# Forward transform of a Fourier layer: row differences moved to GpSimd, table scalings to ScalarE, table pieces handed out anew

## The chip, the cores and the metric

The kernel runs on one core of a Trainium2 chip, in one launch. The metric is the device time of the whole launch in microseconds. Its instructions go to five engines, each with a queue of its own that is worked off strictly in order: TensorE (PE, matmuls; PEld is its weight load), VectorE (DVE), ScalarE (ACT), GpSimd (POOL) and SyncE (SP), which only issues DMAs. All data are 32-bit floats.

## The reference

The input `x` has 16 images of 16 channels of 256 x 256. Two residual layers follow each other. The change lies in the first one, which, cut to its core, is this:

```python
x = x + _L0_conv_ref(_gn(x), ...)          # group norm over 8 groups, then:
alpha = jnp.fft.fft2(x, axes=(-2, -1))
A  = 1.0 / (omega1[:, None, None, None] - weights_pole1[None])   # [256, 16, 16, 4]
Bm = 1.0 / (omega2[:, None, None, None] - weights_pole2[None])
S  = jnp.einsum('ikpq,oikp,xikq->oxik', weights_residue, A, Bm)
output_residue1 = jnp.einsum('biox,oxik->bkox', alpha, S)
C  = jnp.einsum('biox,oikp->bikpx', alpha, A)
D  = jnp.einsum('bikpx,xikq->bikpq', C, Bm)
output_residue2 = jnp.einsum('bikpq,ikpq->bkpq', D, weights_residue)
x1 = jnp.fft.ifft2(output_residue1, ...).real
E1 = jnp.exp(weights_pole1[..., None] * tyc)   # and E2 alike; x2 is built from them
return x1 + x2 / Nx / Ny
```

The second layer is an involution block with a 3 x 3 convolution and a channel gate. It takes most of the time and is untouched.

## The kernel before, in words

The kernel works in four stages, one after the other, with their intermediate results in device memory: `layer0_forward` (group norm, forward Fourier transform, products with the poles), `layer0_mix` (mixing of channels for each frequency), `layer0_back` (inverse transform) and `layer1`. Only `layer0_forward` and what it calls are changed.

**Steps.** `layer0_forward` goes through 64 steps (b, cg): 16 images, and in each 4 groups of 4 channels. In a step,

- `fetch` (two steps ahead) loads 4 channels, 1 MB, to `z`, and takes their statistics on VectorE (`bn_stats`, L174).
- `halves` (one step ahead) forms the group norm's scalars. They cross engines several times: TensorE averages over partitions (`gn_mean`, L34), VectorE does small operations (L36 to L39), TensorE averages again (`gn_var`, L42), then VectorE and ScalarE (square root, L46) make the scale. `eo` is the sum and the difference of the image's upper and lower half: the sum on VectorE (L191), the difference on GpSimd (L194, 128 x 1024).
- `rows`, called twice for two channels each, multiplies `eo` with the Fourier matrix `fy` (L207, into PSUM tile `pu`) and with the pole table `at` (L214, into `pv`). `pu` holds four products, for the left and right half of x and for even and odd frequencies. Left plus right and left minus right go to the two halves of `u`: ScalarE copies the right half to SBUF (`right`, L222), and VectorE adds and subtracts (L224, twice a channel). `u` keeps a whole image, with channels innermost, so each of these writes steps by 64 bytes. There are two `u`, one for the image being filled, one being read.
- `poles` multiplies with `bt` and the residues; `columns`, for the image before, transforms along x (L313), evicts on ScalarE (`o`, L320), and stores to `al` with DMAs issued from GpSimd (L329). `finish` closes an image.

**Tables.** `table` builds `at` before step 0 and `bt` in it. For each half of the channels it forms e = omega - Im(pole) on VectorE (L135, `q`), squares it, adds `p2` (the pole's real part squared, made by GpSimd, L131), takes the reciprocal and multiplies. `tables` builds what the later stages read, and stores it: 16 residue tables (`td`, with 8 matmuls each, L437), 33 plane tables (`avd`) and 16 pieces of exponentials (`ed`, two poles each; sine on ScalarE, exponential by a polynomial on VectorE). `tables` is a generator. `layer0_forward` calls it once at the end of each step from step 4 on; a call issues one residue table, or three planes, or one piece of exponentials, in this order, and the generator is spent before the steps are.

**Who sets the order.** In `layer0_forward` TensorE's order is the one in which the program is written (`manual_schedule` with PE alone). For VectorE, ScalarE, GpSimd and SP a planner places each instruction, using its own estimates of durations and of readiness; so an instruction can stand much earlier in its queue than in the text. In the later stages the order of the compute engines is written by hand. Most tiles of `tables` have one buffer (pools `tc` and `tp`), and PSUM tiles `pu`, `pv` and `px` have two each.

Of the kernel before, what the change touches and what calls it, by code (L numbers as in the profile page):

```python
# [10 lines left out]
F32 = mybir.dt.float32  # L11
I32 = mybir.dt.int32
AF = mybir.ActivationFunctionType
# [5 lines left out]
C = 16  # L19
# [4 lines left out]
M = 4  # L24
# [48 lines left out]
def layer0_forward(ctx, tc, d, al, bd, tabs):  # L73
# [47 lines left out]
    def table(axis, wx, w):  # L121

        t, planes = (at, (0, 1)) if axis == "1" else (bt, (1, 2, 0))
        for half in range(2):
# [5 lines left out]
            p2 = ap.tile([P, 512], F32, tag="p2", name="p2")  # L130
            nc.gpsimd.tensor_tensor(p2, pr, pr, ALU.mult)  # L131
            q = ap.tile([P, 2, 2, 512], F32, tag="q", name="q", bufs=2)
            for h in range(2):
                e, r = q[:, h, 1], q[:, h, 0]
                nc.vector.tensor_scalar(e, pi, -1.0, w[:, h : h + 1], ALU.mult, ALU.add)  # L135
                nc.vector.tensor_tensor(r, e, e, ALU.mult)
                nc.vector.tensor_tensor(r, r, p2, ALU.add)
                nc.vector.reciprocal(r, r)
                nc.vector.scalar_tensor_tensor(e, e, -1.0, r, ALU.mult, ALU.mult)
                nc.vector.scalar_tensor_tensor(r, pr, -1.0, r, ALU.mult, ALU.mult)  # L140
# [56 lines left out]
    def rows(b, cg, j, eo, rs):  # L197
# [3 lines left out]
        for a in range(2):  # L201
# [19 lines left out]
            right = ep.tile([P, 2, 2, 64], F32, tag="right", name="right")  # L221
            nc.scalar.copy(right, pu[:, 1])  # L222
            for h, sign in ((0, ALU.add), (1, ALU.subtract)):
                nc.vector.tensor_tensor(  # L224
                    u[:, h, :, :64, :, ch],
                    pu[:, 0].rearrange("p e v m -> p v m e"),
                    right.rearrange("p e v m -> p v m e"),
                    sign,
                )
# [106 lines left out]
    with tc.manual_schedule(engines={mybir.EngineType.PE}):  # L336
# [6 lines left out]
        for i, (b, cg) in enumerate(steps):  # L343
# [21 lines left out]
            if i >= 4:  # L365
                next(pieces, None)
# [16 lines left out]
def tables(ctx, tc, d, psum, tabs):  # L383
# [5 lines left out]


    krow = load(nc, cp, d["krow_t"], [P, N], "krow_t")
    w = frequencies(nc, cp, d["tx"], krow, [P, N], "wt")
    sign = load(nc, cp, d["sign_t"], [P, 1], "sign_t")
    qr = cp.tile([P, C], F32, name="tqr")
    qi = cp.tile([P, C], F32, name="tqi")
    rr = cp.tile([P, C, M], F32, name="trr")
    ri = cp.tile([P, C, M], F32, name="tri")
    for t in range(2):
        ps = slice(64 * t, 64 * t + 64)
        nc.sync.dma_start(out=qr[ps], in_=d["p2r_iq"])  # L400
        nc.sync.dma_start(out=qi[ps], in_=d["p2i_iq"])
        nc.sync.dma_start(out=rr[ps], in_=d["rr_iq"])
        nc.sync.dma_start(out=ri[ps], in_=d["ri_iq"])
    nc.vector.tensor_scalar(qi, qi, sign, None, ALU.mult)
    nri = cp.tile([P, C, M], F32, name="tnri")
    nc.vector.tensor_scalar(nri, ri, sign, None, ALU.mult)
    nc.vector.tensor_scalar(ri, nri, -1.0, None, ALU.mult)
    q2 = cp.tile([P, C], F32, name="tq2")
    nc.vector.tensor_tensor(q2, qr, qr, ALU.mult)
    mt = load(nc, cp, d["mt"], [P, 2, 16], "mt")  # L410
    for k in range(C):
        e = tp.tile([P, N], F32, tag="te", name="te")
        r = tp.tile([P, N], F32, tag="trec", name="trec")
        br = tp.tile([P, N], F32, tag="tbr", name="tbr")
        nc.vector.tensor_scalar(e, w, qi[:, k : k + 1], None, ALU.add)
        nc.vector.tensor_tensor(r, e, e, ALU.mult)
        nc.vector.tensor_scalar(r, r, q2[:, k : k + 1], None, ALU.add)
        nc.vector.reciprocal(r, r)
        nc.vector.tensor_scalar(br, r, qr[:, k : k + 1], -1.0, ALU.mult, ALU.mult)
        nc.vector.scalar_tensor_tensor(e, e, -1.0, r, ALU.mult, ALU.mult)  # L420
        wts = []
        for h in range(2):
            wt = tp.tile([P, 2, 2, 16, M], F32, tag=f"wt{h}", name="wt")
            shape = [P, 16, M]
            for part, c, coef in ((0, 0, rr), (0, 1, ri), (1, 0, nri), (1, 1, rr)):
                nc.vector.tensor_tensor(
                    wt[:, part, c],
                    mt[:, h].unsqueeze(2).to_broadcast(shape),
                    coef[:, k].unsqueeze(1).to_broadcast(shape),
                    ALU.mult,  # L430
                )
            wts.append(wt)
        yield
        ps = psum.tile([P, 2, N], F32, tag="px", name="pt")
        for h, wt in enumerate(wts):
            for part, rhs in ((0, br), (1, e)):
                nc.tensor.matmul(  # L437
                    ps[:, h],
                    lhsT=wt[:, part].rearrange("p c i m -> p (c i m)"),
                    rhs=rhs,  # L440
                    start=part == 0,
                    stop=part == 1,
                )
        t = tp.tile([P, 2, N], F32, tag="tt", name="tt")
        nc.scalar.copy(t, ps)
        nc.sync.dma_start(out=td[:, :, k], in_=t)

    krow = load(nc, cp, d["krow_m"], [P, N], "krow_m")  # L450
    w = frequencies(nc, cp, d["ty"], krow, [P, N], "wm")
    sign = load(nc, cp, d["sign_m"], [P, 1], "sign_m")
    pr = cp.tile([P, 32], F32, name="tpr")
    pi = cp.tile([P, 32], F32, name="tpi")
    for q in range(4):
        nc.sync.dma_start(out=pr[32 * q : 32 * q + 32], in_=d["p1r_ip"])
        nc.sync.dma_start(out=pi[32 * q : 32 * q + 32], in_=d["p1i_ip"])
    nc.vector.tensor_scalar(pi, pi, sign, None, ALU.mult)
    pr2 = cp.tile([P, 32], F32, name="tpr2")
    nc.vector.tensor_tensor(pr2, pr, pr, ALU.mult)  # L460
    npr = cp.tile([P, 32], F32, name="tnpr")
    nc.vector.tensor_scalar(npr, pr, -1.0, None, ALU.mult)
    for g in range(NF):
        four = [P, 32, 4]
        e = tp.tile(four, F32, tag="ae", name="ae")
        nc.vector.tensor_tensor(
            e,
            w[:, 4 * g : 4 * g + 4].unsqueeze(1).to_broadcast(four),
            pi.unsqueeze(2).to_broadcast(four),
            ALU.add,  # L470
        )
        r = tp.tile(four, F32, tag="ar", name="ar")
        nc.vector.tensor_tensor(r, e, e, ALU.mult)
        nc.vector.tensor_tensor(r, r, pr2.unsqueeze(2).to_broadcast(four), ALU.add)
        nc.vector.reciprocal(r, r)
        av = tp.tile([P, 32, 4, 3], F32, tag="av", name="av")
        half = [64, 32, 4]
        nprb = npr.unsqueeze(2)
        nc.vector.tensor_tensor(av[:64, :, :, 1], r[:64], nprb[:64].to_broadcast(half), ALU.mult)
        nc.vector.tensor_tensor(av[64:, :, :, 1], r[64:], e[64:], ALU.mult)  # L480
        nc.vector.scalar_tensor_tensor(
            av[:64, :, :, 0].rearrange("p k f -> p (k f)"),
            e[:64].rearrange("p k f -> p (k f)"),
            -1.0,
            r[:64].rearrange("p k f -> p (k f)"),
            ALU.mult,
            ALU.mult,
        )
        nc.vector.tensor_tensor(av[64:, :, :, 0], r[64:], nprb[64:].to_broadcast(half), ALU.mult)
        nc.vector.tensor_scalar(av[:, :, :, 2], av[:, :, :, 0], -1.0, None, ALU.mult)  # L490
        nc.sync.dma_start(out=avd[g], in_=av.rearrange("p k f l -> p (k f l)"))
        if g % 3 == 2:
            yield


    phase = load(nc, cp, d["phase"], [P, 1], "phase")
    turn = cp.tile([P, 1], F32, name="turn")
    nc.vector.tensor_scalar(turn, phase, TWO_PI, None, ALU.mult)
    last = load(nc, cp, d["last"], [P, 1], "last")
    c1 = 6.28125  # L500
    c2 = float(np.float32(TWO_PI - c1))
    for i, axis in enumerate("12"):
        pr = cp.tile([P, C], F32, name=f"epr{axis}")
        pi = cp.tile([P, C], F32, name=f"epi{axis}")
        for a in range(2):
            nc.sync.dma_start(out=pr[64 * a : 64 * a + 64], in_=d[f"p{axis}r_kp"])
            nc.sync.dma_start(out=pi[64 * a : 64 * a + 64], in_=d[f"p{axis}i_kp"])
        tr = cp.tile([P, N], F32, name=f"etr{axis}")
        nc.sync.dma_start(out=tr, in_=d["ty" if axis == "1" else "tx"].to_broadcast([P, N]))
        for k in range(0, C, 2):  # L510
            arg = tp.tile([P, 2, N], F32, tag="arg", name="arg")
            n = tp.tile([P, 2, N], F32, tag="n", name="n")
            nf, af = n.rearrange("p k x -> p (k x)"), arg.rearrange("p k x -> p (k x)")
            for j in range(2):
                nc.vector.tensor_scalar(arg[:, j], tr, pi[:, k + j : k + j + 1], None, ALU.mult)
# [979 lines left out]
```

## Time and profile before

| | us |
|---|---|
| median of 3 runs (7382.54 to 7390.2) | 7388.45 |
| the profiled execution, its own time | 7392.98 |
| span of its profile, first to last instruction | 7391.2 |

| engine | busy us | share of the span | instructions |
|---|---|---|---|
| PE (matmul) | 6831.1 | 92% | 57640 |
| PEld (weight load) | 3890.3 | 53% | 57640 |
| VectorE | 4961.8 | 67% | 9441 |
| ScalarE | 3806.5 | 51% | 5915 |
| GpSimd | 3475.6 | 47% | 4636 |

The profile is one execution of the program. Its page gives the busy time of each engine, and groups instructions by line and tile, with the mean duration of one, the idle time of the engine ahead of them, and who ended that idle time. Windows give the busy time in a stretch of the span, with the number of instructions in brackets, then the granted TensorE clock (1.00 is full speed), the share of DMA engines that were busy and GB/s. An instruction's line shows its least, median and greatest duration in ns. In the waits view a line gives who waited for whom, the total, the number of times and the longest, in us. The forward stage is the first 1408 us of the span.

### The profile page before, as it was taken

Reading aid. Unit: us, or ns where it says so; the run is one execution under the profiler, and the core shown is the slowest. Engines: PE = TensorE matmul, PEld = TensorE weight load, DVE = VectorE, ACT = ScalarE, POOL = GpSimd, SP = SyncE. Lnnn points to the kernel's source line nnn. Section 1 sums busy time; section 2 is a strip of 40 time slices with the busy share of each in tenths; the row PEclk is TensorE's granted clock in tenths of the full one; section 3 lists DMA queues with packets and bytes.
Section 4 is the critical chain, followed back from the end, with each engine's and each line's share of the span. In section 5 each row is a group of like instructions: output and inputs, shape, how many; then the busy total and the mean of one; then the engine's idle time right before and its main releaser. Section 6 shows DMA issues by size and latency. Waiting matters only on the chain.

```text
span 7391.2 us, 147380 instructions
## 1 busy us (share of the span) xinstructions
PE 6831.1 (92%) x57640; PEld 3890.3 (53%) x57640; DVE 4961.8 (67%) x9441; ACT 3806.5 (51%) x5915; POOL 3475.6 (47%) x4636
## 2 busy tenths in 40 slices
PE   7889999799999999899789999999999999999996
PEld 5778888566666666677423333333333333333332
DVE  8999975366666666788676656665666666666662
ACT  2223333366666666222366656666666666656662
POOL 2334444322222222566554655555665565655554
PEclk9899999899999999999889999999999999999999
DMA  3444444333333332899767888888888888888886
GB/s 99 111 117 119 118 124 117 109 95 97 98 98 98 98 98 83 305 326 326 249 181 221 259 242 253 252 258 254 253 253 251 256 249 267 256 247 251 256 265 205
DMA packets 716089, 1443.59 MB, mean 195 GB/s; under 512 B 98954, under 2 KB 525254, under 8 KB 673638
## 3 DMA queue, kind: packets, MB, share of 16 engines
q1 hardware_dynamic: 567206, 959.76, 43.4%
q0 software_dynamic: 148192, 474.40, 20.6%
q8 instruction: 460, 7.54, 0.4%
q14 instruction: 231, 1.89, 0.1%
HBM read 877.12 MB, written 556.47 MB: 194 GB/s over the span
## 4 chain that ended last, share of the span: by engine, by line
PE 64%; DVE 7%; ACT 4%; issue 3%; DMA 2%; POOL 0%; SPq 0%; DVEq 0%; ACTq 0%; POOLq 0%
PE c2ps L1169 17%; PE c L1027 12%; PE pd L1095 12%; PE ph L698 5%; PE ps L641 5%; PE pg L663 4%; ACT wide L1075 3%; DVE alb L600 2%; PE pr L1054 2%; PE py L858 2%; PE py L859 2%; PE pt L679 1%; DVE zb L890 1%; DVE st L875 1%; DMA rows<-cf 1%
## 5 line engine op out<-in xcount | busy, mean ns | idle before, releaser
L1075 ACT ACTIVATE wide<-c,b 32x512 f32<-32x512 f32 x2176 | 1477.4, 679 | 354.6 <-PE c L1027 302.8
L1103 DVE TENSOR_TENSOR t<-pd,r 64x512 f32<-64x512 f32 x1088 | 744.3, 684 | 1295.9 <-PE pd L1095 1270.3
L1106 DVE TENSOR_TENSOR top<-pd,t 32x512 f32<-32x512 f32 x2176 | 1504.2, 691 | 52.6
L1169 PE MATMUL c2ps<-rows,c 128*32 128x512 f32 x12288 | 1395.3, 601 | 26.6 <-ACT e L1178 13.7
L1087 POOL COPY wide<-wide 32x1031 f32<-32x1031 f32 (+1 forms) x576 | 568.9, 988 | 1239.0 <-ACT wide L1075 1211.7
L1027 PE MATMUL c<-z,w 102*128 102x512 f32 x2048 | 1014.2, 628 | 138.5 <-ACT wide L1075 115.4
L1095 PE MATMUL pd<-wide,dw 128*128 128x512 f32 x2048 | 1012.5, 616 | 6.4 <-ACT r L1063 2.5
L1169 PEld LDWEIGHTS c2ps<-rows,c 128*32 128x32 f32 x12288 | 393.0, 109 | 993.6 <-issue 885.3
L718 POOL DMA_DIRECT2D hd<-h x512 | 323.5, 639 | 1227.6 <-DVE h L711 1203.5
L1027 PEld LDWEIGHTS c<-z,w 102*128 102x128 f32 x2048 | 401.2, 198 | 675.9 <-issue 486.0
L1095 PEld LDWEIGHTS pd<-wide,dw 128*128 128x128 f32 x2048 | 376.8, 194 | 614.3 <-issue 449.0
L1178 ACT ACTIVATE e<-c2ps,b 128x512 f32<-128x512 f32 x256 | 175.9, 687 | 845.6 <-PE c2ps L1169 842.9
L1088 POOL COPY wide<-wide 32x1031 f32<-32x1031 f32 (+1 forms) x576 | 572.2, 993 | 35.8
L313 PE MATMUL px<-wxn,u 128*64 128x256 f32 x4224 | 557.8, 385 | 2.2 <-ACT o L320 2.1
L641 PE MATMUL ps<-tt,lt 128*64 128x256 f32 x4224 | 495.5, 384 | 38.9 <-DVE lt L627 35.9
L698 PE MATMUL ph<-ix,yt 64*128 64x256 f32 x4128 | 502.5, 391 | 5.4 <-issue 4.7
L313 PEld LDWEIGHTS px<-wxn,u 128*64 128x64 f32 x4224 | 400.7, 136 | 127.0 <-ACT o L320 5.1
L698 PEld LDWEIGHTS ph<-ix,yt 64*128 64x128 f32 x4128 | 392.7, 190 | 91.7 <-issue 44.6
L1046 ACT ACTIVATE bot<-c,b 128x512 f32<-128x512 f32 x544 | 344.1, 684 | 175.7 <-PE c L1027 168.2
L207 PE MATMUL pu<-fy,eo 128*128 128x128 f32 x2048 | 425.5, 291 | 6.0 <-DVE u L224 4.4
L320 ACT ACTIVATE o<-px,rsc 128x512 f32<-128x512 f32 (+1 forms) x272 | 186.0, 686 | 472.2 <-PE px L313 441.1
L871 POOL TENSOR_TENSOR x<-x,o 128x512 f32<-128x512 f32 x256 | 324.0, 1266 | 216.7 <-DVE o L870 215.3
(203 smaller groups left out, 10818.5 us busy)
## 6 DMA issues: line engine op xcount, KB each, us to landing
rows<-cf SPq DMA_DIRECT2D x128, 2176.0 KB
z<-zn SPq DMA_DIRECT2D x768, 257.8 KB
cf<-top POOLq DMA_DIRECT2D x512, 240.0 KB, 7.1
cf<-bot POOLq DMA_DIRECT2D x96, 840.0 KB, 11.6
alc<-al SPq DMA_DIRECT2D x264, 256.0 KB
zn<-zb SPq DMA_DIRECT2D x128, 516.0 KB
o<-zn SPq DMA_DIRECT2D x128, 516.0 KB
z<-in_x SPq DMA_DIRECT2D x64, 1024.0 KB
```

What stands on the lines that cost most here:

```text
L207: nc.tensor.matmul(pu[:, xh, e].rearrange("p v m -> p (v m)"), lhsT=lhs, rhs=fy[:, e], start=True, stop=True,)
L313: nc.tensor.matmul(ps[64 * k : 64 * k + 64, :, h], lhsT=u[:, h, part, g0 + j + k].rearrange("p f c -> p (f c)"), rhs=wxn[:, h, part], star ...
L641: nc.tensor.matmul(ps[64 * h : 64 * h + 64, v], lhsT=lt[:, h, k, 1 - v : 3 - v].rearrange("p l f c -> p (l f c)"), rhs=tt[:, h, k], start= ...
L698: nc.tensor.matmul(ph[q][:, e], lhsT=yt[lanes, i].rearrange("p t k -> p (t k)"), rhs=ix[lanes, i], start=n == 0, stop=n == 3,)
L1027: nc.tensor.matmul(ps[:, a], lhsT=w, rhs=z[:k, c : c + 2, 0:N], start=True, stop=True)
L1075: nc.scalar.activation(self.feat[64 - 32 * q : 96 - 32 * q, f, self.groups[g], :H], ps[q][32 * f : 32 * f + 32], AF.Mish, bias=b1[0][32 * ...
L1087: nc.gpsimd.tensor_copy(flat[0:32, f, 1:m], flat[64:96, f, 0 : m - 1])
L1088: nc.gpsimd.tensor_copy(flat[96:128, f, 0 : m - 1], flat[32:64, f, 1:m])
L1095: nc.tensor.matmul(ps, lhsT=dwt if self.tail else dw, rhs=self.feat[:, f, cs, :H], start=True, stop=True,)
L1103: nc.vector.tensor_tensor(t[64:128], ps[:64], self.r[:, cs], ALU.mult)
L1106: nc.vector.tensor_tensor(self.top[32 * f : 32 * f + 32, cs, q], ps[lanes], t[lanes], ALU.add)
L1169: nc.tensor.matmul(ps[32 * j : 32 * j + 32], lhsT=c2[:, blk, dx, :], rhs=t[:, 4 * j + blk : 4 * j + blk + 4, x : x + H], start=(blk, dx) = ...
```

## The change

It has three parts, all in the forward stage.

1. In `rows`, ScalarE copies all of `pu` (both halves, 512 columns) to a new SBUF tile `both` with three buffers. VectorE adds from it, and GpSimd subtracts from it. `pu` is read by ScalarE alone.
2. Scalings and additions of a per-partition value move from VectorE to ScalarE: e in `table`; three operations of each residue table; the negation of a plane; in the exponentials the products with the poles' parts and, for the second axis, with `last`. A plane's addition and square (`ae`, `ar`) move from VectorE to GpSimd. In `table`, `p2` is written over `pi` once ScalarE has read that.
3. `tables` becomes three generators (residues, planes, exponentials) whose 16 + 33 + 16 = 65 pieces are interleaved by their relative positions. A call issues one piece, a plane counting as one. From step 4 on each step makes one call, and steps 4, 16, 28, 40 and 52 make two, so the calls last to step 63.

```diff
@@ table
-            p2 = ap.tile([P, 512], F32, tag="p2", name="p2")
-            nc.gpsimd.tensor_tensor(p2, pr, pr, ALU.mult)
             q = ap.tile([P, 2, 2, 512], F32, tag="q", name="q", bufs=2)
             for h in range(2):
+                nc.scalar.activation(q[:, h, 1], pi, AF.Identity, bias=w[:, h : h + 1], scale=-1.0)
+            p2 = pi
+            nc.gpsimd.tensor_tensor(p2, pr, pr, ALU.mult)
+            for h in range(2):
                 e, r = q[:, h, 1], q[:, h, 0]
-                nc.vector.tensor_scalar(e, pi, -1.0, w[:, h : h + 1], ALU.mult, ALU.add)
@@ rows
-            right = ep.tile([P, 2, 2, 64], F32, tag="right", name="right")
-            nc.scalar.copy(right, pu[:, 1])
-            for h, sign in ((0, ALU.add), (1, ALU.subtract)):
-                nc.vector.tensor_tensor(
-                    u[:, h, :, :64, :, ch],
-                    pu[:, 0].rearrange("p e v m -> p v m e"),
-                    right.rearrange("p e v m -> p v m e"),
-                    sign,
-                )
+            both = ep.tile([P, 2, 2, 2, 64], F32, tag="both", name="both", bufs=3)
+            nc.scalar.copy(both, pu)
+            left, right = (both[:, i].rearrange("p e v m -> p v m e") for i in range(2))
+            nc.vector.tensor_tensor(u[:, 0, :, :64, :, ch], left, right, ALU.add)
+            nc.gpsimd.tensor_tensor(u[:, 1, :, :64, :, ch], left, right, ALU.subtract)
@@ layer0_forward, end of a step
-            if i >= 4:
+            for _ in range(0 if i < 4 else 2 if i % 12 == 4 else 1):
                 next(pieces, None)
@@ tables, residues
-        nc.vector.tensor_scalar(e, w, qi[:, k : k + 1], None, ALU.add)
+            nc.scalar.activation(e, w, AF.Identity, bias=qi[:, k : k + 1])
             nc.vector.tensor_tensor(r, e, e, ALU.mult)
-        nc.vector.tensor_scalar(r, r, q2[:, k : k + 1], None, ALU.add)
+            nc.scalar.activation(r, r, AF.Identity, bias=q2[:, k : k + 1])
             nc.vector.reciprocal(r, r)
-        nc.vector.tensor_scalar(br, r, qr[:, k : k + 1], -1.0, ALU.mult, ALU.mult)
+            nc.scalar.activation(br, r, AF.Copy, scale=nqr[:, k : k + 1])
@@ tables, planes
-        nc.vector.tensor_tensor(
+            nc.gpsimd.tensor_tensor(
                 e,
...
-        nc.vector.tensor_tensor(r, e, e, ALU.mult)
+            nc.gpsimd.tensor_tensor(r, e, e, ALU.mult)
...
-        nc.vector.tensor_scalar(av[:, :, :, 2], av[:, :, :, 0], -1.0, None, ALU.mult)
+            nc.scalar.activation(av[:, :, :, 2], av[:, :, :, 0], AF.Copy, scale=-1.0)
             nc.sync.dma_start(out=avd[g], in_=av.rearrange("p k f l -> p (k f l)"))
-        if g % 3 == 2:
-            yield
+            yield
@@ tables, exponentials (pr and, for the second axis, last alike)
-                nc.vector.tensor_scalar(arg[:, j], tr, pi[:, k + j : k + j + 1], None, ALU.mult)
+                    nc.scalar.activation(arg[:, j], tr, AF.Copy, scale=pi[:, k + j : k + j + 1])
@@ tables, end
+    parts = ((residues(), C), (planes(), NF), (exponentials(), C))
+    order = sorted(((i + 0.5) / n, p) for p, (_, n) in enumerate(parts) for i in range(n))
+    for _, p in order:
+        next(parts[p][0])
+        yield
+    for part, _ in parts:
+        for _ in part:
+            pass
```

In the built program VectorE has 482 instructions fewer (8959), ScalarE 161 more, GpSimd 322 more; TensorE and SP have as many as before.

## The prediction

> **What bounds the kernel now.** The change touches only the forward stage, so I first look for that stage's end. On the timeline the last `columns` matmul ends at 1408 us, and the mixing stage starts its matmuls at 1443. The order of all later instructions is the same in both programs on every engine, so the 5980 us after 1408 are taken as fixed.
>
> I cut the forward stage where its work changes: steps 4 to 20, in which `tables` issues residues and planes; steps 21 to 45, with exponentials alone; steps 46 to 62, without tables. The first view is the busy time by stage, the second the same for the row matmuls (L207) alone, 32 to a step, which counts the steps.
>
> ```profile
> core 0: us, PE busy (x) PEld busy (x) DVE busy (x) ACT busy (x) POOL busy (x), PEclk, DMA share, GB/s
> ...
> 140.80:564.60 423.80, 377.25 (x3010) 329.83 (x3010) 388.82 (x1160) 117.79 (x217) 155.52 (x212) 0.92 0.41 113
> 564.60:1042.00 477.40, 470.71 (x4223) 405.33 (x4222) 441.18 (x1125) 180.62 (x319) 227.94 (x312) 1.00 0.45 120
> 1042.00:1355.50 313.50, 313.50 (x2868) 273.05 (x2867) 165.88 (x517) 96.24 (x191) 149.48 (x211) 1.00 0.41 108
> ```
> ```profile
> 140.80:564.60 423.80, 124.91 (x544) 98.65 (x545) 0.92 0.41 113
> 564.60:1042.00 477.40, 158.85 (x800) 121.39 (x801) 1.00 0.45 120
> 1042.00:1355.50 313.50, 108.01 (x544) 82.55 (x544) 1.00 0.41 108
> ```
>
> 17, 25 and 17 steps: 24.9, 19.1 and 18.44 us each. In the last group TensorE never rests, so 18.44 is its own pace. The first group loses 423.8 - 313.5 = 110 us against it. The tables' own matmuls (L437, 128 of them, 31.9 us by the windows of that line) explain a part; 78 us are lost. Who is waited for there says the waits view of that group:
>
> ```profile
> PE gn_var L42 <- DVE gnq L39: 44.5, 15, 4.7
> ...
> PE pu L207 <- DVE u L224: 0.7, 4, 0.2
> ```
>
> TensorE waits for the group norm's small VectorE operations (L36 to L39), which stand in VectorE's queue behind the tables' work; VectorE is busy 92% of that group. The other 32 us come with the lower clock (0.92; row matmuls of 317 ns there against 280 in the next group). So VectorE sets steps 4 to 20, TensorE the rest. Group 2 loses only 477.4 - 25 x 18.44 = 16 us, with VectorE just as busy (92%); its excess falls on steps with a Sin, which brings table loads of 1283 ns to ScalarE.
>
> **What the Trainium skill says.** "SBUF — State Buffer", section "Who interferes with whom": a VectorE instruction with two SBUF inputs, or in a two-port mode, contends with a GpSimd instruction that reads SBUF, and the second to come waits for the first to end. The trace agrees: L224, with one PSUM input, never stretches, while short SBUF operations are at times held for over a microsecond:
>
> ```profile
> L224 DVE TENSOR_TENSOR u<-pu,right x504: 569/591/619, 108.6 to 1363.7; 128x256 f32<-128x256 f32 x168
> ```
> ```profile
> L473 DVE TENSOR_TENSOR ar<-ae x33: 277/283/1427, 157.7 to 536.7; 128x128 f32<-128x128 f32 x33
> ```
>
> "GPSIMD Engine Reference", section "3.1 Elementwise — side-by-side cycle accounting": about 2.6 cycles an element for two inputs, that is 2.2 ns at its 1.2 GHz; the rows here give (2366 - 726) ns / 768 elements = 2.1 (L194, L265). "ScalarE: Activation LUTs", section "What ACT_TABLE_LOAD costs": 186 ns + 0.833 ns an element, 93 ns more for a per-partition operand; L231 (512 elements, one such operand) took 692 ns against 706.
>
> **The change, part by part.** Durations are from the one profiled execution: 7392.98 us, its span 7391.2; the median of the three runs is 7388.45, 0.06% lower. I subtract from the median.
>
> *Row differences.* Of 8 L224 in a step, 4 leave VectorE. Two in a row take 1.04 us, so 4 x 0.52 = 2.1 us a step. The 4 adds that stay now read two SBUF operands: nearest row L711, same size with contiguous operands, 415 ns, against 591; so -0.17 each, or more than 591 where GpSimd holds the port. I leave them at 591. ScalarE's copy grows from 256 to 512 columns: 371 to 585 ns (L445), +0.86 us a step. It now frees `pu` without VectorE, a wait worth 4.4 us in all (L207 row of the page). GpSimd gets 4 subtractions: 726 ns contiguous (L265), and 1.04 us if the step-64-byte writes cost as they do VectorE (591/415 = 1.43); so 2.9 to 4.2 us a step onto its 149.48/17 = 8.8.
>
> *Tables.* VectorE's base in group 3 is 165.88/17 = 9.76 us a step. So tables cost it 388.8 - 17 x 9.76 = 223 in group 1 and 441.2 - 25 x 9.76 = 197 in group 2: 420 us. To ScalarE go 3 x 16 residue operations (0.36 us), 33 negations L490 (0.36), 64 scalings L515/L525 (0.35) and 8 of L528 (0.48); to GpSimd 2 x 33 (L466 0.305, L473 0.36). Sum 17 + 12 + 22 + 4 + 22 = 77 us; operations overlap by some 0.06 us, 219 of them, so 63 net. 357 us stay. ScalarE gets by the skill's price 0.49 us for 256 columns: an estimate of 70 us in all, over half a hundred steps, onto 7.2 a step; it ends near 10 of 19 and is covered by TensorE's pace. GpSimd ends near 14 of 19.
>
> *Spreading.* Here I don't believe the words. The hand-written order binds TensorE alone; in the changed program's VectorE order, planes stand in steps 4 to 27 and exponentials in 6 to 34, as early as the planner could put them. Only residues, whose buffers wait for matmuls, are spread: one in four steps to step 63, 8 of the 16 after step 34. A residue piece is 0.42 + 1.74 + 0.42 + 8 x 0.21 = 4.2, net 3.6 us. So steps 4 to 34 hold 357 - 8 x 3.6 = 328 us of tables, 10.6 a step, with a base of 9.76 - 2.05 = 7.7: **18.3 us**, where TensorE wants 18.44 + 8 x 2.0/31 = 18.96, and some 0.6 more for Sin's table loads: 19.5. VectorE is almost level with it, not clear of it.
>
> *Steps 4 to 34.* Before:
>
> ```profile
> 140.80:831.70 690.90, 639.94 (x5366) 556.18 (x5365) 638.08 (x1795) 218.93 (x396) 281.67 (x385) 0.95 0.42 116
> ```
>
> At best 31 x 19.5 = 605, a gain of 86. Add 0.4 us for collisions with the subtractions and hold VectorE at the 92% at which it ran when it was the bound: 18.7/0.92 = 20.3, times 31 = 629: gain **62**, which I take. With 2 us of collisions and of new VectorE-ScalarE-VectorE hops (a residue's square, add, reciprocal, scaling now alternate; behind ScalarE's waiting instruction stand the `pu` copies and `o` evictions that TensorE needs) 22.1 x 31 = 685: gain 6.
>
> *Steps 35 to 62.* Before 523.8 us, 28 x 18.44 = 516.3 and 7.5 of excess. After: no excess, but 8 residue pieces of 2.0 us of matmuls: **loss 8.5**. The last `td` store moves to the end of step 63; the final `columns` (33 us of matmuls from 1374.6) cover it, since SP asks for `tt` at 1409.6. Without that cover it would cost a few us. Setup loads on SP are the same in number and lie beside prefetched steps: nothing.
>
> *Start.* The eight L135 leave VectorE, but its reciprocals wait for `p2`, and that for `pr`'s DMA (VectorE idle until 38.58, released by GpSimd's L131): no gain. `p2` written over `pi` delays `pi`'s next load by about 2.4 us, still far ahead of `pr`'s. A 1.2 us gap of the table matmuls near 89 us and 1.6 us of waiting in steps 1 to 3 may go: 0 to 5, I take **3**.
>
> Sum: 62 - 8.5 + 3 = 56 us. 7388.45 - 56 is about 7332.
>
> **Rivals.** (a) TensorE bound throughout (port collisions rare, adds at 415 ns): 86 - 8.5 + 3 = 80, 7308. For it: group 2 ran so with VectorE at 92%; against: the bunching. (b) The gain is eaten by hops and collisions: 6 - 8.5 + 3, about 7388, spread over 7364 to 7400. For it: stretched rows such as L473. (c) Slower: GpSimd becomes the bound. With 8.8 us of its own a step and 0.5 for planes, it exceeds TensorE at 2.3 us a subtraction, and the 20.6 us that steps 4 to 63 took on average at 2.8 us. At 3.5 us: 60 x (23.3 - 20.6) = 162 slower, 7550. No row shows a GpSimd operation with 64-byte steps; against it speaks the 0.73 to 1.04 above.
>
> **How the numbers follow.** 7332 case 0.64 (own range 7310 to 7364), (a) 0.15, (b) 0.12, (c) 0.09. Under 0.2% (15 us, about what a measurement of this kernel can tell from no change) fall two thirds of (b): same 0.08; faster 0.64 + 0.15 + 0.04 = 0.83; slower 0.09. The range 7300 to 7374 leaves out (c) and most of (b).
>
> **What would show it.** Right: the wait of L42 for L39 shrinks to under 15 us; steps 4 to 34 take 605 to 650 us with clock near 1; the L224 line halves and VectorE's forward work drops by some 190 us; steps 35 on slightly longer; subtractions at 0.7 to 1.1 us. Wrong: GpSimd subtractions above 2 us, adds stretched beyond 800 ns, TensorE waiting for the `both` copy behind ScalarE's tables, or a wider gap at 1408 to 1443.

## The result, and the profile after

The changed kernel takes 7497.72 us (median of four runs, 7488.39 to 7506.78) against 7385.49 for the kernel before beside it: a ratio of 1.0155 (95% interval 1.0136 to 1.0174), so 1.6% **slower**. The forecast was 0.8% faster. The profiled execution of after took 7499.75 us, its span is 7498.0, 106.8 more than before's.

The steps are counted by the row matmuls as in the prediction (L208 now). The last `columns` matmul ends at 1507 us instead of 1408, which is 99 of those 106.8 us; so nearly all of it lies in the forward stage. Windows of after, for steps 4 to 34 and 35 to 62 (columns as in the prediction's first view):

```profile
core 0: us, PE busy (x) PEld busy (x) DVE busy (x) ACT busy (x) POOL busy (x), PEclk, DMA share, GB/s
...
150.50:915.90 765.40, 656.54 (x5293) 555.53 (x5294) 701.29 (x1500) 297.32 (x526) 479.15 (x572) 0.93 0.36 103
915.90:1453.80 537.90, 536.11 (x4796) 467.58 (x4795) 330.64 (x833) 196.98 (x347) 384.19 (x461) 1.00 0.41 111
```

| stage | before, us | after, us | difference |
|---|---|---|---|
| to step 4 | 140.8 | 150.5 | +9.7 |
| steps 4 to 34 | 690.9 | 765.4 | +74.5 |
| steps 35 to 62 | 523.8 | 537.9 | +14.1 |

The first line of the windows (steps 4 to 34) is the strange one. Before, VectorE had 1795 instructions and 638.08 us of work in steps 4 to 34. Now it has 1500 instructions and **701.29 us**. It lost a sixth of its instructions and got busier. So its remaining instructions must have become longer, and the line view by form shows which. VectorE in steps 4 to 34 of after (busy us, mean ns of one, then idle time ahead of it), and below it the same group-norm lines of before:

```profile
L225 DVE TENSOR_TENSOR u<-both 128x256 f32<-128x256 f32 x125 | 108.4, 869 | 3.1 <-ACT both L223 2.8
L52 DVE TENSOR_SCALAR gnt<-gnt 128x2 f32<-128x2 f32 x31 | 31.3, 1009 | 0.1
L51 DVE TENSOR_TENSOR gnt<-gnt,gnv 128x2 f32<-128x2 f32 x31 | 22.0, 709 | 0.2
L39 DVE TENSOR_TENSOR gnq<-gnq,mv 128x2 f32<-128x2 f32 x31 | 15.6, 503 | 0.0
```
```profile
L52 DVE TENSOR_SCALAR gnt<-gnt 128x2 f32<-128x2 f32 x31 | 14.0, 450 | 0.0
L51 DVE TENSOR_TENSOR gnt<-gnt,gnv 128x2 f32<-128x2 f32 x31 | 10.2, 329 | 0.0
L39 DVE TENSOR_TENSOR gnq<-gnq,mv 128x2 f32<-128x2 f32 x31 | 4.7, 153 | 0.0
```

These are operations on two elements a partition. The median of L52 is 157 ns in both kernels; a few long ones make its mean: 4 of the 31 took over 1 us before, 12 in after. The instruction lines give the spread (least, median, greatest ns), here for the adds and the subtractions of after:

```profile
L225 DVE TENSOR_TENSOR u<-both x256: 519/600/5880, 68.9 to 1461.7; 128x256 f32<-128x256 f32 x128
```
```profile
L226 POOL TENSOR_TENSOR u<-both x256: 1067/1142/3567, 69.0 to 1461.7; 128x256 f32<-128x256 f32 x128
```

An add takes 0.6 us and one took 5.88. Most adds are not held: in steps 4 to 34 one in six (21 of 124) lasted over 0.8 us, and these make the mean of 869. The timeline shows what it was doing (start and duration in us; lines of VectorE and GpSimd):

```profile
610.62 3.59 POOL L226 TENSOR_TENSOR u<-both 128x256 f32<-128x256 f32 x3
611.04 1.19 DVE L780 TENSOR_SCALAR exp_n<-exp_n 128x512 f32<-128x512 f32 x1
612.15 5.88 DVE L225 TENSOR_TENSOR u<-both 128x256 f32<-128x256 f32 x1
614.18 2.34 POOL L195 TENSOR_TENSOR eo<-z 128x1024 f32<-128x1024 f32 x1
616.48 1.08 POOL L226 TENSOR_TENSOR u<-both 128x256 f32<-128x256 f32 x1
617.88 0.67 DVE L783 SCALAR_TENSOR_TENSOR arg<-exp_n,arg 128x512 f32<-128x512 f32 x1
```

The add starts at 612.15, while GpSimd is in the second of three subtractions, and ends at 618.03, half a microsecond after GpSimd's last one ends (616.48 + 1.08 = 617.56). Until then GpSimd went on to a third subtraction, to `eo` and to a fourth subtraction without a pause: each starts 0.03 to 0.04 us before the one ahead of it ends (614.18 against 610.62 + 3.59 = 614.21, for one). The add was not let in between; it was held through four instructions. It isn't always so: L780, of 0.43 us when nothing holds it, waits behind the first subtraction and ends at 612.23, 0.3 us into the second one, which had followed without a pause too.

I use one sum for all kernels below, called the **stretch**: over VectorE's instructions from step 0 to step 63, the time by which each is longer than the tenth percentile of its own form. It is 117 us before and 305 after (a few us hang on how the percentile is taken), while the rest of the durations fell from some 1170 to 960. Of the stretch, the small operations of the group norm have 141 us (38 before) and the row adds 67 (6 before).

TensorE's waits in steps 4 to 34 of after (who waited for whom; total us, times, longest):

```profile
PE gn_var L42 <- DVE gnq L39: 43.1, 13, 7.4
PE px L310 <- ACT o L317: 35.4, 14, 3.8
PE pd L238 <- ACT v L228: 15.5, 6, 7.1
```

L42's wait has not gone (44.5 before), and the two for ScalarE are new but for 1 us. TensorE idles 765.4 - 656.5 = 109 us there, 51 before. The other 16.6 us are TensorE's own: it has 73 matmuls fewer there (8 residue tables now come later) and is busy longer all the same, at a mean clock of 0.93, 0.95 before.

### The profile page after: what moved, and what is told of

It is laid out like the page before. It is cut to its first block, busy times and chain, and to the rows that moved or that the text cites. A ratio compares the mean times of both kernels' runs of the same rounds, so it can differ in the third digit from the quotient of the medians.

```text
span 7498.0 us, 147335 instructions
## 1 busy us (share of the span) xinstructions
PE 6874.9 (92%) x57640; PEld 3915.0 (52%) x57640; DVE 5003.5 (67%) x8959; ACT 3918.2 (52%) x6076; POOL 3832.4 (51%) x4958
## 4 chain that ended last, share of the span: by engine, by line
PE 62%; DVE 7%; issue 4%; ACT 4%; DMA 2%; POOL 1%; SPq 0%; DVEq 0%; ACTq 0%; POOLq 0%
PE c2ps L1180 17%; PE c L1038 12%; PE pd L1106 12%; PE ph L709 5%; PE ps L652 5%; PE pg L674 4%; ACT wide L1086 3%; DVE alb L611 2%; PE pr L1065 2%; PE py L869 2%; PE py L870 1%; PE pt L690 1%; DVE zb L901 1%; DVE st L886 1%; DMA rows<-cf 1%
## 5 line engine op out<-in xcount | busy, mean ns | idle before, releaser
L310 PE MATMUL px<-wxn,u 128*64 128x256 f32 x4224 | 581.7, 394 | 35.4 <-ACT o L317 35.4
L208 PE MATMUL pu<-fy,eo 128*128 128x128 f32 x2048 | 423.0, 290 | 7.8 <-ACT both L223 7.7
L611 DVE TENSOR_SCALAR alb<-alc,m 128x1024 f32<-128x1024 f32 x330 | 420.2, 1397 | 0.0
```

The source lines that it names most:

```text
L310: nc.tensor.matmul(ps[64 * k : 64 * k + 64, :, h], lhsT=u[:, h, part, g0 + j + k].rearrange("p f c -> p (f c)"), rhs=wxn[:, h, part], star ...
L611: eng.tensor_scalar(dst, t, m4[:, j : j + 1], None, ALU.mult)
```

## The experiments

All ratios are to the kernel before, run on the same chip beside them. Theory P, the one I began with, was that VectorE's operations are held while GpSimd works.

### Which part of the change costs

**rows_only**: the changed `rows` and `table`, with before's `tables` and its calls.

```diff
-            for _ in range(0 if i < 4 else 2 if i % 12 == 4 else 1):
+            if i >= 4:
                 next(pieces, None)
```

> The kernel before with the changed rows and table functions (copy of both halves by ScalarE, addition on VectorE, subtraction on GpSimd); the pieces of tables and their order are those of before. Theory P (port): GpSimd's subtractions hold the SBUF port that VectorE's two-input and two-port operations also need, VectorE's operations stretch, and since it sets the pace the stage gets longer: 60 to 150 us slower than before, 7450 to 7535. Theory H (hops): the loss comes from the tables' new ScalarE-VectorE-ScalarE hops, which are absent here: 7340 to 7390. Theory B (bunching of the interleaved pieces): 7340 to 7390 too.

7536.77, ratio 1.0204 (1.0188 to 1.0219).

**tables_only**: the changed kernel with before's `rows`.

```diff
-            nc.scalar.copy(both, pu)
...
+            nc.scalar.copy(right, pu[:, 1])
+            for h, sign in ((0, ALU.add), (1, ALU.subtract)):
...
```

> The changed kernel with the rows function of before (copy of the right half, addition and subtraction on VectorE, one operand in PSUM). Theory P: without the subtractions on GpSimd the relief of VectorE (some 63 us of work) shows: 7320 to 7365. Theory H: the hops are all there: 7450 to 7500. Theory B: the pieces stand as in the changed kernel: 7450 to 7500.

7371.02, 0.9979 (0.997 to 0.9988).

**sub_vector**: the changed kernel, one word different.

```diff
-            nc.gpsimd.tensor_tensor(u[:, 1, :, :64, :, ch], left, right, ALU.subtract)
+            nc.vector.tensor_tensor(u[:, 1, :, :64, :, ch], left, right, ALU.subtract)
```

> The changed kernel with its subtraction on VectorE instead of GpSimd; both operands still come from the SBUF copy. Theory P: VectorE has 2.1 us more a step and two operands in SBUF, but GpSimd's port traffic is back to that of before: 7340 to 7395. Theories H and B: little changes or it gets worse with the added VectorE work: 7480 to 7560.

7393.76, 1.0004 (0.9995 to 1.0013).

The loss is in the rows, and in the rows it is the engine of the subtraction. The wider copy, its third buffer, the tables on ScalarE and the new order together cost nothing against before. (Against tables_only they cost 0.25%: so the wider copy and the operands in SBUF have a price of their own, with a stretch of 152 us against 105.) Giving VectorE 256 operations more makes the kernel 1.5% faster than after; the mean of L39 in steps 4 to 34 is 151 ns then, as before.

**sub_half**: of the two channels in a call of `rows`, one subtracts on GpSimd and one on VectorE.

```diff
+            eng = nc.vector if a else nc.gpsimd
-            nc.gpsimd.tensor_tensor(u[:, 1, :, :64, :, ch], left, right, ALU.subtract)
+            eng.tensor_tensor(u[:, 1, :, :64, :, ch], left, right, ALU.subtract)
```

> The changed kernel with the subtraction on GpSimd for the first channel of each pair and on VectorE for the second. Theory P with a loss in proportion to GpSimd's work: half way between the kernel with all subtractions on VectorE (7394) and the changed one (7498): 7430 to 7460. If collisions grow only when GpSimd runs several operations in a row: near 7400 to 7420. If the loss is a wait for GpSimd's last subtraction in a step: near 7394.

7448.76, 1.0069 (1.0054 to 1.0084): a little under half of the way from 1.0004 to 1.0155. The loss goes with the number of subtractions on GpSimd.

### Is it the holding, or the longer way of the data?

**sub_memset** (a miss).

```diff
-            nc.gpsimd.tensor_tensor(u[:, 1, :, :64, :, ch], left, right, ALU.subtract)
+            for _ in range(3):
+                nc.gpsimd.memset(u[:, 1, :, :64, :, ch], 0.0)
```

> The changed kernel with each subtraction on GpSimd replaced by three GpSimd memsets of the same part of u, so the differences are left out; GpSimd is about as long busy, waits for the same buffers of u, but reads no SBUF. Theory P: the collisions with VectorE's two-input operations go: 7320 to 7370. A theory in which GpSimd's mere occupation or its late work is to blame, or H or B: 7450 to 7500.

7539.17, 1.0206 (1.0191 to 1.0222), where theory P gave 7320 to 7370. Memsets wait for no data, so the planner put them in long rows on GpSimd, and VectorE's `tensor_scalar` operations on two elements got longer than in after. In its stretch from 150 to 900 us, nearly its steps 4 to 34 (162.5 to 929.5):

```profile
L52 DVE TENSOR_SCALAR gnt<-gnt 128x2 f32<-128x2 f32 x30 | 42.4, 1414 | 0.1
```

So writes alone hold this form, and my idea that only GpSimd's reads matter fell. As a test of the reads it is spoiled by the moved instructions, which also make step 0 start at 86.0 us instead of 65.0.

**left_psum**: VectorE takes the left operand of its add from PSUM, as before; GpSimd still subtracts.

```diff
-            nc.vector.tensor_tensor(u[:, 0, :, :64, :, ch], left, right, ALU.add)
+            nc.vector.tensor_tensor(u[:, 0, :, :64, :, ch], pu[:, 0].rearrange("p e v m -> p v m e"), right, ALU.add)
```

> The changed kernel with the addition's left operand read from PSUM, so that the addition has one SBUF operand and can't collide; the subtraction stays on GpSimd. Theory P: the additions' own stretching goes (37 us of VectorE time in steps 4 to 34), the others' stays: 7450 to 7485. If the collision of addition and subtraction, started by the same copy, is the whole of it: 7380 to 7420. Freeing pu later, by VectorE, may cost some of it again.

7465.7, 1.009 (1.0075 to 1.0105). VectorE in its steps 4 to 34:

```profile
L225 DVE TENSOR_TENSOR u<-pu,both 128x256 f32<-128x256 f32 x125 | 73.4, 589 | 18.8 <-ACT both L223 18.6
L52 DVE TENSOR_SCALAR gnt<-gnt 128x2 f32<-128x2 f32 x31 | 16.6, 536 | 0.2
L39 DVE TENSOR_TENSOR gnq<-gnq,mv 128x2 f32<-128x2 f32 x31 | 14.2, 459 | 0.0
```

One operand moved to another memory, and the add is back at 589 ns from 869. 0.65 of the 1.76 per cent between tables_only and after go with it, though the add now holds `pu` longer (TensorE waits 42.9 us for it in the forward stage). The group norm's L39 is still held, but all its small operations together are held less (78 us of stretch, 141 in after), so the 0.65% are not the adds' own stretch alone.

**sub_unused**: tables_only, and beside it one subtraction a channel on GpSimd that nobody reads; the copy `right` has three buffers here and in the next three (two in tables_only).

```diff
+            unused = ep.tile([P, 2, 64, 2], F32, tag="unused", name="unused")
+            both = right.rearrange("p e v m -> p v m e")
+            nc.gpsimd.tensor_tensor(unused, both, both, ALU.subtract)
```

> The kernel with the changed tables and the rows of before (7371 measured), where GpSimd subtracts the copied half from itself once a channel into a scratch tile that nobody reads; the copy has three buffers. No instruction on the path waits for these results. Theory P (port): GpSimd's reads alone stretch VectorE's operations: 7420 to 7490. A theory in which the changed kernel loses because its data wait for GpSimd's late subtractions: 7360 to 7385.

7412.58, 1.002 (1.0013 to 1.0027): 0.41% above tables_only, a quarter of after's 1.76%. Both theories missed. Two things differ from after. These subtractions are shorter (mean 0.71 us, after's 1.22), and they run while VectorE has its own operations with a PSUM operand, which stay at 590 ns.

**sub_unused_spaced** was to make them longer, by spaced writes.

```diff
-            unused = ep.tile([P, 2, 64, 2], F32, tag="unused", name="unused")
+            unused = ep.tile([P, 2, 64, 2, 3], F32, tag="unused", name="unused", bufs=1)
-            nc.gpsimd.tensor_tensor(unused, both, both, ALU.subtract)
+            nc.gpsimd.tensor_tensor(unused[..., ch % 3], both, both, ALU.subtract)
```

> Tables as in the changed kernel, rows as in the kernel before (VectorE makes sums and differences from PSUM), and beside them one GpSimd subtraction of the same size for each channel, from the copy of the right half into a scratch tile that nobody reads, with spaced writes (every third word) instead of the contiguous ones of the earlier version (714 ns, 7412.6 us). Nobody waits for it. If spaced writes make it last 1.1 to 1.2 us as in the changed kernel, theory P (VectorE is held while GpSimd works) gives 7371 + 41 x 1.17/0.71 = 7440, range 7420 to 7480. Theory D (the loss is the longer way of the data from TensorE over ScalarE and GpSimd to u): no more than the 7405 to 7420 of the contiguous version.

7407.92, 1.0018 (1.001 to 1.0025). A step of 12 bytes costs GpSimd nothing (0.71 us again), so the condition in the expectation was not met, and this only repeats sub_unused.

**sub_unused_double**: two of them a channel.

```diff
+            for _ in range(2):
                 nc.gpsimd.tensor_tensor(unused, both, both, ALU.subtract)
```

> As the first unread version (7412.6 us against 7371 without), but two unread GpSimd subtractions after each channel: 1.43 us of GpSimd work a channel, more than the 1.22 us of the changed kernel's subtraction, in short runs. Theory W (amount of work): 7371 + 2 x 41 = 7453, 7435 to 7470. Theory R (length of the runs): runs are at most 1.4 us, 3.8 where eo follows, so less than double the loss, 7410 to 7432.

7439.66, 1.0071 (1.0054 to 1.0087). 

**sub_unused_run**: the four of a step in a row after its fourth channel (behind the loop over channels).

```diff
+        if j:
+            for _ in range(4):
                 nc.gpsimd.tensor_tensor(unused, both, both, ALU.subtract)
```

> Rows of the kernel before, tables of the changed one, and the four unread GpSimd subtractions of a step (0.71 us each, contiguous scratch, read from the copy of the right half) issued in a row after its fourth channel instead of one after each channel. Same GpSimd work as the unread version that took 7412.6 us. Theory R (a VectorE operation that is held stays held until an unbroken run of GpSimd instructions ends): runs of 2.9 us, 5.3 us where eo follows, so VectorE operations held for over 2 us several times as often, 7430 to 7470. Theory W (the loss goes with the amount of GpSimd's work): 7405 to 7420 as before.

7391.36, 1.0006 (0.9999 to 1.0013). I had it the wrong way round: the same work in a row costs no more, rather less, and twice the work costs about twice. (A row also stands elsewhere in the step and so meets other VectorE operations; that was not told apart.) In the row GpSimd leaves a gap of 0.08 us between two of these subtractions (median of 192 in the trace; the four write one tile, which may be why, and was not tested), and VectorE gets in. The timeline of sub_unused_run:

```profile
387.11 2.36 POOL L195 TENSOR_TENSOR eo<-z 128x1024 f32<-128x1024 f32 x1 [0.72 <-PE pv L215]
387.26 2.23 DVE L53 TENSOR_TENSOR rs<-gnr,gnt 128x2 f32<-128x2 f32 x1
389.41 0.68 DVE L530 SCALAR_TENSOR_TENSOR arg<-n,arg 128x512 f32<-128x512 f32 x1
389.44 3.57 POOL L235 TENSOR_TENSOR unused<-right 128x256 f32<-128x256 f32 x4
390.02 0.71 DVE L485 TENSOR_TENSOR ar<-ar,tpr 128x128 f32<-128x128 f32 x1
...
391.53 1.00 DVE L531 SCALAR_TENSOR_TENSOR arg<-n,arg 128x512 f32<-128x512 f32 x1
```

`eo` (2.36 us) holds L53 to its end. Beside the four subtractions L485 and L531 lose only 0.4 and 0.3 us. But a gap is not what VectorE needs: L53 got in although the first of the four had started (389.44) before `eo` ended (389.47), as L780 did in after. I counted this in after, steps 0 to 63, for the VectorE operations that lasted over 0.2 us longer than the tenth percentile of their form. They stood waiting at 126 ends of a GpSimd instruction that another followed without a gap. At 94 VectorE got in, and the next GpSimd instruction lasted 0.26 us longer (median); at 32, in 19 operations of 245, it was passed over. What decides between the two is not shown. So a hold mostly ends with one GpSimd instruction, and sometimes goes on through several. None of the unread versions has an operation stretched by over 2.5 us; after has 12, which carry 53 of its 305 us.

The unread versions have the same VectorE work as tables_only (some 1103 us without the stretch), which makes them a scale for it:

| kernel | above tables_only | stretch, us |
|---|---|---|
| tables_only | 0 | 105 |
| sub_unused_run | 0.27% = 20 us | 123 |
| sub_unused | 0.41% = 30 us | 145 |
| sub_unused_double | 0.92% = 68 us | 180 |
| left_psum | 1.11% = 82 us | 205 |
| after | 1.76% = 130 us | 305 |

About one us is lost for each us of stretch (18, 40 and 75 against 20, 30 and 68), though nobody waits for GpSimd's result. The ratios leave 8 to 14 us of doubt in each loss, so this is a rough scale from three kernels. In the last two rows VectorE has 142 us less work of its own, and they lose 82 and 130 us all the same.

**after_eo_vector** takes the longest member out of GpSimd's rows in the changed kernel.

```diff
-        nc.gpsimd.tensor_tensor(eo[:, 1], z[:, :, 0], z[:, :, 1], ALU.subtract)
+        nc.vector.tensor_tensor(eo[:, 1], z[:, :, 0], z[:, :, 1], ALU.subtract)
```

> The changed kernel with one operation more on VectorE: the difference of halves eo (128x1024, 2.55 us on GpSimd, once a step, and part of most of GpSimd's runs of over 4 us) goes from GpSimd to VectorE, where it should take some 1.4 us (twice L192's 0.7 us for 512). Theory R: holds of over 4 us are gone, and VectorE gains more than the 64 x 1.4 = 90 us that it takes on: 7400 to 7460. Rival V (VectorE has too much work in steps 4 to 34, whatever holds it): 7500 to 7550.

7427.01, 1.0059 (1.0041 to 1.0077): 1% faster than after, with 64 operations of 1.25 us more on VectorE, its fullest engine. Stretch 211 us, adds at 738 ns. VectorE's amount of work is not what makes the changed kernel slow.

### Is it the bunching?

**tables_gated** and **after_gated** hold a step's pieces behind that step's rows.

```diff
-                next(pieces, None)
+                with tc.issue_after(marks["dve"].ins), tc.issue_after(marks["act"].ins):
+                    next(pieces, None)
```

(`marks` keeps the last row add and the last eviction of `v`.) tables_gated has before's rows:

> Changed tables, rows of before (7371 measured), and each piece of the tables held on VectorE and ScalarE behind the last instruction of rows in its step, so that pieces really stand in steps 4 to 63. Theory B (bunching): VectorE has 9.8 + 6 us of work a step against TensorE's 18.4, TensorE sets the pace: 7300 to 7335. If bunching costs nothing, because port collisions or hops are what is left: 7360 to 7385.

7362.02, 0.9952 (0.9936 to 0.9969): 0.27% under tables_only, but far from theory B's range and inside the other one. after_gated is the changed kernel with it:

> The changed kernel, with one difference: the pieces of tables issued in a step are held on VectorE and ScalarE behind that step's last row add and last eviction of v, so that they can't bunch in steps 4 to 34. The same gate took 0.27% from the version whose rows are those of the kernel before (7371 to 7362 in its own call, 33 us less by the profiles' stage to step 35). Theory P (VectorE's operations are held while GpSimd works on the subtractions, wherever the pieces stand): the collisions stay and only the queue ahead of TensorE gets shorter, 7440 to 7480, with adds still above 700 ns in steps 4 to 34. Theory B (the bunching is the cause: subtractions on GpSimd are harmless where VectorE has slack): 7350 to 7395, at or below the kernel before, adds near 600 ns.

7494.14, 1.0139 (1.0121 to 1.0157), above theory P's range and not to be told from after. The gate spreads the pieces in fact: the last plane is stored at 1463 us, in after at 709. Steps 4 to 34 then take 687.4 us, but 35 to 62 take 613.8 (537.9 in after), so the collisions are only dealt out over all steps (the stretch is 343 us in all). VectorE is busy for 84% of steps 4 to 34 (575.90 of 687.4), no longer full, and TensorE still waits. One case, on the timeline of after_gated:

```profile
363.00 2.37 POOL L327 DMA_DIRECT2D al<-o  x4 [3.45 <-ACT o L318]
...
364.79 6.35 DVE L782 TENSOR_SCALAR exp_n<-exp_n 128x512 f32<-128x512 f32 x1
365.35 3.20 POOL L227 TENSOR_TENSOR u<-both 128x256 f32<-128x256 f32 x3
...
368.49 2.35 POOL L196 TENSOR_TENSOR eo<-z 128x1024 f32<-128x1024 f32 x1
...
372.80 0.15 DVE L44 TENSOR_SCALAR gnv<-gn_var 128x2 f32<-128x2 f32 x1
...
372.98 0.20 ACT L46 ACTIVATE gnr<-gnv 128x2 f32<-128x2 f32 x1 [5.15 <-DVE gnv L44]
...
374.30 2.24 PE L239 MATMUL pd<-bt,v 128*64 128x128 f32 x13 [4.93 <-ACT v L229]
```

This is how one hold reaches TensorE. L782 needs 0.43 us and takes 6.35. It starts while GpSimd issues stores, and ends 0.3 us after `eo`, the fourth computing instruction that GpSimd has put behind them. L44 stands behind it on VectorE, ScalarE's L46 waits 5.15 us for L44, behind L46 stand the copies and the eviction of `v`, and TensorE waits 4.93 us for `v`.

**spread_gated** has before's engines throughout (every operation of the change's second part back where it was), with the new order of pieces and the gate.

```diff
-            nc.scalar.activation(e, w, AF.Identity, bias=qi[:, k : k + 1])
+            nc.vector.tensor_scalar(e, w, qi[:, k : k + 1], None, ALU.add)
...
```

> The kernel before with its own engines throughout (no work moved to ScalarE or GpSimd), but with the pieces of tables in the changed kernel's interleaved order and held behind each step's rows as in the gated versions. Theory S (what the tables' part gains, it gains by the spreading): as the gated version with the scalings on ScalarE, 7355 to 7375. Theory A (it gains by taking 63 us of scalings from VectorE): 7380 to 7400.

7360.9, 0.9955 (0.9938 to 0.9972).

**tables_gated_pv** is tables_gated with a plane's two operations back on VectorE.

```diff
-            nc.gpsimd.tensor_tensor(r, e, e, ALU.mult)
+            nc.vector.tensor_tensor(r, e, e, ALU.mult)
```

(and `ae` alike)

> The fastest version so far (7362: rows of the kernel before, tables' scalings on ScalarE, pieces held behind each step's rows), with the two operations of a plane that the change moved to GpSimd put back on VectorE. Theory P: the 66 operations on GpSimd (0.5 us each) hold VectorE about as long as they relieve it (66 x 0.33 = 22 us), and both are spread over 60 steps that TensorE mostly sets: 7350 to 7368. Rival (VectorE is still the bound in the gated steps, and 22 us more of work show): 7372 to 7390.

7357.17, 0.9956 (0.9941 to 0.9971). The three gated versions with before's rows beat both kernels, by 0.45% within each other's intervals. The spreading makes this gain (new order and gate together; the gate with before's order was not run); taking the scalings from VectorE adds nothing that can be told once it is there. Steps 4 to 34 of spread_gated:

```profile
137.10:763.80 626.70, 598.62 (x5294) 518.57 (x5293) 536.52 (x1498) 205.73 (x379) 289.90 (x385) 0.99 0.43 118
```

The clock is 0.99, and its 5294 matmuls are busy 598.6 us, in after 656.5 for 5293. Steps 35 to 62, to which half of the pieces went, take 562.9 us (523.8 before); so step 63 starts 28.8 us earlier than before.

## Why the prediction was wrong, point by point

**The bound.** That VectorE's queue sets steps 4 to 20, and that time is lost there, fits spread_gated, which gains 0.45% by moving no work but its place in the queue. How much was to be had is another matter. spread_gated has 626.7 us for steps 4 to 34, where I forecast 629, but that is luck: it has fewer pieces there, and pays for them in steps 35 to 62. The fastest version (tables_gated_pv) is 37 us below before; no run shows the 56 that I forecast.

**The step that failed**: "Add 0.4 us for collisions with the subtractions and hold VectorE at the 92% at which it ran when it was the bound: 18.7/0.92". The second half held: VectorE was busy 701.29/765.4 = 92%. The first did not. 701.29/31 is 22.6 us a step, not 18.7; 22.6/0.92 is 24.6, and 24.7 were measured. Stretch alone grew from 78 to 196 us in these steps (2.5 to 6.3 a step), so the collisions added 3.8 us, not 0.4; that is the term that was mis-sized. I had taken "never stretches" from the old L224, which has a PSUM operand, and gave the new add, which has none, its 591 ns with a word of caution. It is released by the same copy as the subtraction, so the two can collide: the adds last 0.28 us longer on average, by one in six that is held. The larger part is the group norm's small operations (141 us of stretch, 38 before), which the sum left out though TensorE waits for them. I had also read "waits for the first to end" in the Trainium skill, "SBUF — State Buffer", "Who interferes with whom", as one GpSimd instruction. The page says that the port is taken for a whole instruction. The trace agrees with this at 94 of the 126 ends counted above and goes beyond it at 32: an L784 of 7.59 us was held through five in a row. The page also ties only the case of two SBUF inputs to GpSimd's reads, and not two-port modes, which I ran together. That L52 was held beside memsets (1414 ns) would fit the second; no run shows in which mode it works.

**Sizes beside it.** The subtraction takes 1.14 us at the median, just outside 0.73 to 1.04; GpSimd is busy 479.15/31 = 15.5 us a step ("near 14"), ScalarE 9.6 ("near 10"). These were good enough, and beside the point: neither engine was full.

**Steps 35 to 62**: loss of 14.1, forecast 8.5. The 16 us of residue matmuls are there (TensorE is busy 536.11 of 537.9 us). Of the 5.6 us that the forecast was short, 5 are a step of 18.25 us instead of 18.07 wherever ScalarE copies `both` (sub_half, left_psum and sub_vector too); what makes it was not tested.

**Start**: forecast a gain of 3, measured a loss of 9.7, most of it in step 0 (45.4 us, 40.7 before) and step 3 (17.7, 10.3 before). tables_only is at 141.0 at step 4, as before; sub_unused at 145.9, sub_unused_double at 149.8. So this too comes with GpSimd's subtractions, but not with them alone: after_gated and after_eo_vector have all four on GpSimd and are at 142.0 and 140.5.

**Spreading disbelieved**: right. The last plane is stored at 709 us, in step 26, the last sine runs at 855, in step 31. I didn't see that this part, if enforced, was all the gain that any run here has.

**After 1408 us**: taken as fixed; 8 us of the 106.8 lie there, not explained. Executions of before differ by 19 us among themselves.

**Rivals.** (c) had the right sign and the wrong mechanism: GpSimd was to be full at over 2.3 us a subtraction. (b), "2 us of collisions", had the mechanism (with hops, of which tables_only, which has them all, shows no loss) at half its size, 22.1 us a step. Of the signs I listed, "adds stretched beyond 800 ns" came true (869).

**What stays open.** after loses 130 us to tables_only, and unread subtractions of somewhat more GpSimd time (sub_unused_double, 622 us against 606) lose 68. The rest is not divided up. Taking the adds out of the collision gives 48 us back (left_psum). Another part may be the longer way of the data: ScalarE waits for GpSimd to free `both` (51 us in left_psum), and sub_vector, with the copy but without GpSimd, is 0.25% above tables_only. A version in which GpSimd's result is needed but nothing is held was not found.

## What to carry to other kernels

Before moving work from VectorE to GpSimd, look at what VectorE does at that moment. If it is released by the same event and reads two SBUF operands, the two can collide (here one add in six, and none with an operand in PSUM), and short operations on TensorE's path are held behind GpSimd too. Charge the move with the stretch that a trace shows for such operations (here 3.8 us a step for some 3 us of VectorE work removed), and expect a few holds far longer than one GpSimd instruction. Where one engine's side work bunches ahead of the critical operations, hold it behind them first: with the pieces in the new order that alone gave 0.45%, with no work moved.

## What the runs showed of the hardware that I had not expected

- A VectorE operation can be held through several GpSimd instructions that follow each other without a gap: up to 5.88 us for a 0.6-us add, 6.35 for a 0.43-us `tensor_scalar`, 7.59 for a 0.69-us L784. More often it got in at the end of one, also where the next followed without a gap (94 of 126 times in after).
- The hold doesn't go by size: operations on two elements a partition (0.15 us) were at 1.0 us on average (L52).
- GpSimd's subtraction of 256 columns took 1.14 us with writes 64 bytes apart, and 0.62 us (both medians) with contiguous ones or ones 12 bytes apart. The short ones read one operand twice, the long ones two; which of the two differences counts was not tested.
- In spread_gated, tables_only and after, 5293 or 5294 matmuls of steps 4 to 34 were busy 598.6, 607.7 and 656.5 us at mean clocks of 0.99, 0.98 and 0.93, while TensorE stood idle for 28, 43 and 109 us. Idle time alone doesn't set the clock: before was idle for 51 us at 0.95, sub_vector for 51 at 0.98.
